# Moving parts within the instruction queues of a two-layer graph network: walk products ahead of the searches' parts, transposes in one run, loads on another engine, later side work

## The chip, the cores and the metric

The kernel runs on one core of one Trainium2 chip. The time is the device time of one execution in microseconds (us). It was run three times, and the median counts. One further execution was profiled; the profile and its trace come from that one.

## The reference, cut to what matters

A graph of N = 2708 nodes with D = 256 features passes through two layers. `x` is (2708, 256), `adj` (2708, 2708); all is float32.

```python
# layer 0: two steps of attention and of a random walk
R = adj + eye;  R = R / R.sum(-1)
Xf = Xa = x;  Z = 0
for n in range(2):
    q, k = Xa @ W1.T @ W2.T, Xa @ W3.T            # width 64
    probs = softmax(q @ k.T)                      # (2708, 2708)
    A = probs cut to the fewest largest values of a row whose sum reaches 0.9
    A = A / A.sum(-1)
    Xf, Xa = R @ Xf, A @ Xa
    Z = Z + Xf @ U1[n].T + Xa @ U2[n].T
x = layernorm(x + layernorm(x + Z) * g + b)
# layer 1: graph attention of 4 heads, width 64 each
Wh = einsum('nd,hdo->nho', x, W)
e = leaky_relu(s_i[:, None, :] + s_j[None, :, :], 0.2)   # s from Wh and a
att = softmax(where(adj != 0 or i == j, e, -inf), axis=1)
x = layernorm(x + einsum('ijh,jho->iho', att, Wh))
```

## The kernel before, in words

**Tiles.** The rows are cut into 22 tiles (`NT`): 16 of 128 rows and 6 of 110. Tiles of one height are taken in six groups of 4, 4, 4, 4, 4 and 2 (`groups`). TensorE (PE) makes all products; ScalarE (ACT) exponentials, copies and sums; VectorE (DVE) the searches; GpSimd (POOL) small sums; SyncE (SP) starts most DMAs. `manual_schedule` keeps PE, ACT, DVE and POOL in the order in which the program issues, one block for layer 0 and one for layer 1; SP is not among them.

**Opening.** `turn_x` (L1080) transposes x into `x_turned` (which lies in `ba`), group by group: four tiles by two halves c of the features, the halves side by side in one PSUM tile `lg`. ACT copies the half c = 0 and DVE the half c = 1 (L1091). `project` makes the queries and keys (L631) one group behind.

**Steps of layer 0.** A *search* (`search`) finds for one tile of rows which probabilities are kept. It is a generator in parts: `scores` (products L661, exponentials L665), `survey` (tallies on ACT, L686, and POOL), `bound` (a pass of DVE over the row, L751), `candidates` (L766), `settle` (L779-L838; its last pass, L835, leaves the values that the attention product transposes). The first step's searches have no survey. `step(s, ...)` goes through the tiles; for each tile, `weigh` takes the six groups: transposes of the next group (L240), ACT's copy `eT` (L245), products with the values (`att`, L258), and then `between(n)`, which ends in one call of `slot`. So a tile has six slots, n = 0 to 5. In slot 4 the search of the tile three further on is begun.

A slot drives three lists. `going` holds the searches and `doing` the smaller finishing jobs; `advance` takes each a part further. `stream` is the *random walk*, `walks`: 22 products L901 to each tile of R, read in blocks `blk` from HBM. A slot takes a given number of them (`spend`: 7 between the steps, 7 or 6 counted pieces a slot in the second). A walk's 22nd product appends the job `after_walk0` (first step) or `finish` (second step) and runs its first part at once: the DVE add that reads the walk's only PSUM bank (L915 with reciprocal L916, or L974). Its second part, at the next `advance(doing)`, is work for POOL (L918, L919) or ACT (L976) and POOL.

```python
            advance(going)
            if begin and begin[1] < NT:
                ...
            advance(doing)
            owed[0] += spend
            while owed[0] > 0: ...        # the walk's products
```

**Layer 1.** For each pair of a source tile j and a span of 8, 8 or 6 target tiles: the mask (`neighbours`: adj block loaded by SP, then Sign and Square on ACT, L1221/L1222), four weight tiles `pt` on DVE (L1302), products with `v` (L1313) and with the denominators (L1323) on PE. `mask(n)` runs three pairs ahead and `weights(n)` two; in the first span `mask` also loads `v[j]` (L1290). The loop makes two pairs an iteration and calls `beside` twice. `beside` carries side work: the last four tiles of layer 0 (`LATE`), whose layer norms and sources are made by `prepared` (ACT L145, L148, L153, POOL, then transposes L160 and products L166 on PE, exponentials and copies L162-L176 and a DMA L179 on ACT), and `verdict`, a check of the searches. Each of these has a count of calls before it starts.

**Buffers.** Each pool takes a stretch of on-chip memory in the order in which it is opened; layer 1's pools lie over those of layer 0, which are closed.

Of the kernel before, what the change touches and what calls it, by code (L numbers as in the profile page):

```python
# [37 lines left out]
HELD, WAITING = 6, 4  # L38
# [6 lines left out]
def kernel(  # L45
# [16 lines left out]
    nc = tc.nc  # L62
# [5 lines left out]
    NT = (N + P - 1) // P  # L68
# [48 lines left out]
    LATE = 4  # L117
# [37 lines left out]
    def sources(t, pool, room, queue=nc.sync):  # L155

        m = rows[t]
        tp = room()
        for c in range(DC):
            nc.tensor.transpose(tp[:, c, :m], xe[:m, t, c * P : (c + 1) * P], ident[:m, :m])  # L160
        xT = pool.tile([P, DC, P], F32, name="xT")
        nc.scalar.copy(xT[:, :, :m], tp[:, 0:DC, :m])  # L162
        yield
        wp = room().rearrange("p a b -> p (a b)")
        for c in range(DC):
            nc.tensor.matmul(  # L166
                wp[:m, : D + 2 * H], xT[:, c, :m], wx[:, c, :],
                start=(c == 0), stop=(c == DC - 1),
            )
        nc.scalar.activation(sb[:m, t, :], wp[:m, D : D + H], AF.Exp)  # L170
        nc.scalar.activation(tj[:m, t, :], wp[:m, D : D + H], AF.Exp, scale=NEG_SLOPE - 1.0)
        nc.scalar.copy(s_src[:m, t, :], wp[:m, D + H : D + 2 * H])
        vt = pool.tile([P, D], F32, name="cs")
        for h in range(H):
            cols = slice(h * FO, (h + 1) * FO)
            nc.scalar.activation(  # L176
                vt[:m, cols], wp[:m, cols], AF.Copy, scale=sb[:m, t, h : h + 1]
            )
        queue.dma_start(vd[t][:m], vt[:m])  # L179

    def norms(t, xt, norm=layernorm, other=None):

        m = rows[t]
        hh = xe[:m, t, 0:D]
        h2 = hh if other is None else other()[:m]
        yield from norm(h2, hh, m)
        nc.gpsimd.tensor_mul(h2, h2, g_sb[:m])  # L187
        nc.gpsimd.tensor_add(h2, h2, xt[:m])  # L188
        yield
        yield from norm(hh, h2, m)  # L190
        yield
        if t < NT - LATE:
            yield
# [331 lines left out]
    def fast_layer0(ep, adjp):  # L525

        l0 = ExitStack()

        heldp, finp, rowp, w0, keep, tpp, sortp, keepb, wk = (
            l0.enter_context(tc.tile_pool(name=name, bufs=bufs))  # L530
            for name, bufs in (
                ("heldp", HELD), ("finp", 2), ("rowp", 2), ("w0", 1), ("keep", 1),
                ("tpp", 3), ("sortp", 1), ("keepb", 1), ("wk", 1),
            )
        )
        ps_lg, ps_wk, ps_at, ps_tr = (
# [304 lines left out]
        def search(s, t):  # L841

            e, z, tau = yield from scores(s, t)
            if s:
                seen = yield from survey(t, e, z, tau)
                src, rest = bound(t, e, z, tau, *seen)
            else:
                src, rest = e, tau
            yield
            cand = yield from candidates(s, t, src)  # L850
            yield
            ready[t] = e, (yield from settle(s, t, e, cand, rest))
# [138 lines left out]
        stream = walks()  # L991
        owed = [0]

        def advance(parts):
            for g in list(parts):
                if next(g, parts) is parts:
                    parts.remove(g)

        def slot(spend, begin=None):

            advance(going)
            if begin and begin[1] < NT:
                going.append(search(*begin))
                next(going[-1])
            advance(doing)
            owed[0] += spend
            while owed[0] > 0:
                owed[0] -= 1
                if next(stream, True):
                    break  # L1010

        def step(s, cur, spend):
            first = None
            for t in range(NT):
# [11 lines left out]
                def between(n):  # L1026
                    last = n == len(groups) - 1
                    if last:
                        xa = heldp.tile([P, D], F32, name="xa1")
                        nc.scalar.activation(xa[:m], ac[:m, :D], AF.Copy, scale=rden)  # L1030
                        if s and t in c3:
                            nc.gpsimd.dma_start(c3[t][:m], xa[:m])
                            stored.add(t)
                        elif s:
                            held[t] = xa
                        else:
                            doing.append(after_attention0(t, xa))
                    slot(spend[n], (s, t + 3) if n == len(groups) - 2 else None)
# [41 lines left out]
        def turn_x(grp):  # L1080
            k = rows[grp[0]]
            w, c0 = k * len(grp), off[grp[0]]
            tp = ps_lg.tile([P, 2, CHUNK], F32, name="lg")
            for c in range(DC):
                for q, t in enumerate(grp):
                    nc.tensor.transpose(
                        tp[:, c, q * k : (q + 1) * k], xm[:k, t, c * P : (c + 1) * P],
                        ident[:k, :k],
                    )
                copy = nc.vector.tensor_copy if c else nc.scalar.copy  # L1090
                copy(x_turned[:, c, c0 : c0 + w], tp[:, c, :w])  # L1091
            return c0, w

        with tc.manual_schedule(engines=engines):
            query_weights()
            ahead = turn_x(groups[0])
            for n in range(len(groups)):
# [3 lines left out]
                pj = ps_tr.tile([P, 4, P], F32, name="tr").rearrange("p a b -> p (a b)")  # L1101
# [5 lines left out]
            for n in range(10):  # L1107
                slot(0, (0, n // 4) if n in (0, 4, 9) else None)
                for t in range(n * NT // 10, (n + 1) * NT // 10):
                    terms1(t, x_turned[:, :, off[t] : off[t + 1]])  # L1110
            layer1_weights()
            step(0, xm, [0] * len(groups))
            while doing:
                slot(SPEND_BETWEEN)
# [78 lines left out]
    def layer1(ep, adjp, r=None, verdict=None):  # L1193
        l1 = ExitStack()

        pp, pj, rp, keep = (
            l1.enter_context(tc.tile_pool(name=name, bufs=bufs))
            for name, bufs in (("pp", 2), ("pj", 1), ("rp", 1), ("keep1", 1))
        )
        DEEP = 3  # L1200
        ps_u = l1.enter_context(tc.tile_pool(name="ps_u", bufs=2, space=PSUM))
# [12 lines left out]
        def neighbours(g, j):  # L1214

            k = rows[j]
            i0, i1 = off[spans[g][0]], off[spans[g][-1] + 1]
            bar = adjp.tile([P, NT - HT, P], F32, name="blk")
            bar = bar.rearrange("p t d -> p (t d)")[:k, : i1 - i0]
            nc.sync.dma_start(bar, adjT[off[j] : off[j + 1], i0:i1])  # L1220
            nc.scalar.activation(bar, bar, AF.Sign)  # L1221
            nc.scalar.activation(bar, bar, AF.Square)  # L1222
            if j in spans[g]:
                own = bar[:, off[j] - i0 : off[j + 1] - i0]
                nc.vector.tensor_tensor(own, own, ident[:k, :k], op=ALU.max)
            return bar
# [59 lines left out]
        def mask(n):  # L1286
            if n < len(order):
                g, _, j = order[n]
                if g == 0:
                    nc.sync.dma_start(  # L1290
                        v[j][: rows[j]].rearrange("p h o -> p (h o)"), vd[j][: rows[j]]
                    )
                masks[n] = neighbours(g, j)
# [36 lines left out]
        def prepared(t):  # L1330

            yield from norms(
                t, x_late[:, t - NT + LATE, :], layernorm_beside,
                lambda: pp.tile([P, D], F32, name="h2", bufs=4),
            )
            yield from sources(t, pp, aux, nc.scalar)


        late = []
        if verdict:  # L1340
            late += [[k, prepared(NT - LATE + k)] for k in range(LATE)]
            late.append([LATE, verdict(aux)])
        rest, running = [], []
        def beside(g, i):

# [19 lines left out]
        for n in range(DEEP):  # L1365
            mask(n)
# [3 lines left out]
        for n in range(0, len(order), 2):  # L1370
            g, i, j = order[n]
            beside(g, i)
            weights(n + 2)
            mask(n + 3)
            if i == 0:
                acc = [
# [7 lines left out]
            for u in (n, n + 1):  # L1384
                for k in range(2):
                    values(u, (2 * k, 2 * k + 1))
                    if last and u > n:
                        for c, (c0, w) in enumerate(cuts[g]):
                            copy = nc.scalar.copy if c == 0 else nc.vector.tensor_copy
# [3 lines left out]
            if last:  # L1393
                for c, (c0, w) in enumerate(cuts[g]):
                    copy = nc.scalar.copy if c == 0 else nc.vector.tensor_copy
# [3 lines left out]
            else:  # L1399
                beside(g, i + 1)  # L1400
            weights(n + 3)
            mask(n + 4)
        assert not late

# [10 lines left out]
    with ExitStack() as both:  # L1415

        adjp = both.enter_context(tc.tile_pool(name="adjp", bufs=3))
        ep = both.enter_context(tc.tile_pool(name="ep", bufs=3))
        left = fast_layer0(ep, adjp)
        with tc.manual_schedule(engines=engines):  # L1420
            layer1(ep, adjp, *left)
    flag = nc.values_load(bad[0:1, 0:1])
    with tc.If(flag > 0):
        general_layer0()
        with ExitStack() as again:
            adjp = again.enter_context(tc.tile_pool(name="adjp", bufs=3))
            ep = again.enter_context(tc.tile_pool(name="ep", bufs=3))
            layer1(ep, adjp)
# [45 lines left out]
```

## Time and profile before

| What | Value |
|---|---|
| Median of three runs | 1595.95 us (1595.8 to 1597.88) |
| Profiled execution, its own time | 1593.14 us |
| Its span, first to last instruction | 1591.3 us |
| Mean granted TensorE clock | 0.990 |
| Busy: PE / DVE / ACT / POOL | 1542.3 / 1202.5 / 798.9 / 429.1 us |
| Opening to the first scores of layer 0 | about 0 to 34 us |
| First step, then between the steps | to about 446, then to 523 us |
| Second step | 523 to 1229 us |
| Layer 1 | from 1229 us |

The table reads the profiled execution, except for its first row. Busy times overlap, as the engines run beside each other. The page cuts the span in 40 slices of 39.8 us, and a digit gives the busy share of an engine in one. The list of waits puts each idle stretch of an engine down to the work that ended it; a timeline gives start, length, line and tiles of runs of instructions, and in brackets the idle time before them with what ended it. "SPq" and "ACTq" are SP and ACT at starting DMAs.

### The profile page before, as it was taken

Reading aid. Unit: us, or ns where it says so; the run is one execution under the profiler, and the core shown is the slowest. Engines: PE = TensorE matmul, PEld = TensorE weight load, DVE = VectorE, ACT = ScalarE, POOL = GpSimd, SP = SyncE. Lnnn points to the kernel's source line nnn. Section 1 sums busy time; section 2 is a strip of 40 time slices with the busy share of each in tenths; the row PEclk is TensorE's granted clock in tenths of the full one; section 3 lists DMA queues with packets and bytes.
Section 4 is the critical chain, followed back from the end, with each engine's and each line's share of the span. In section 5 each row is a group of like instructions: output and inputs, shape, how many; then the busy total and the mean of one; then the engine's idle time right before and its main releaser. Section 6 shows DMA issues by size and latency. Waiting matters only on the chain. (4 is left out here: it accounts for less than half of the span.)

```text
span 1591.3 us, 23822 instructions
## 1 busy us (share of the span) xinstructions
PE 1542.3 (97%) x8029; PEld 1037.7 (65%) x8029; DVE 1202.5 (76%) x3651; ACT 798.9 (50%) x1462; POOL 429.1 (27%) x884
## 2 busy tenths in 40 slices
PE   6999999999998999999999999999999999999994
PEld 3477777777776888787787788887787333333342
DVE  2777677767408876878779888888884978999995
ACT  2444444444335455555555556556643454456473
POOL 1311000000022222232224454534441720033133
PEclk9999999999999999999999999999999999999997
DMA  5200000000134333333333334433344434334331
GB/s 139 78 13 14 12 9 12 10 9 10 42 94 124 86 100 82 98 76 78 80 102 94 100 107 107 111 104 93 78 101 130 130 102 139 93 105 133 85 100 43
DMA packets 172494, 128.27 MB, mean 81 GB/s; under 512 B 44342, under 2 KB 161804, under 8 KB 172362
## 3 DMA queue, kind: packets, MB, share of 16 engines
q1 hardware_dynamic: 165030, 114.63, 26.9%
q0 software_dynamic: 3648, 9.26, 1.8%
q10 hardware_dynamic: 3684, 2.76, 0.5%
q8 instruction: 65, 1.06, 0.3%
q14 instruction: 67, 0.55, 0.1%
HBM read 111.78 MB, written 13.46 MB: 79 GB/s over the span
## 5 line engine op out<-in xcount | busy, mean ns | idle before, releaser
L245 ACT COPY eT<-tr 128x512 f32<-128x512 f32 (+5 forms) x264 | 141.2, 535 | 275.8 <-PE tr L240 273.1
L686 ACT ACTIVATE junk<-e,minus,rth 128x2708 bf16<-128x2708 f32 (+1 forms) x88 | 232.8, 2646 | 36.1 <-POOL rth L718 35.2
L258 PE MATMUL att<-xm,eT 128*128 128x256 f32 (+3 forms) x968 | 230.9, 380 | 0.4 <-ACT xa L1030 0.4
L258 PE MATMUL att<-ba,eT 128*128 128x256 f32 (+3 forms) x968 | 230.8, 379 | 0.3 <-ACT eT L245 0.2
L901 PE MATMUL walk<-xe,blk 128*128 128x257 f32 (+3 forms) x968 | 225.3, 384 | 5.0 <-DVE xf L915 5.0
L901 PE MATMUL walk<-xm,blk 128*128 128x256 f32 (+3 forms) x968 | 222.0, 380 | 1.0 <-DVE xw L974 1.0
L1313 PE MATMUL acc<-pt,v 128*64 128x512 f32 (+3 forms) x1056 | 216.3, 555 | 2.4 <-DMA v<-v 2.2
L901 PEld LDWEIGHTS walk<-xe,blk 128*128 128x128 f32 (+3 forms) x968 | 178.5, 187 | 50.3 <-issue 12.6
L1302 DVE SCALAR_TENSOR_TENSOR pt<-e,tj,blk 128x1024 f32<-128x1024 f32 (+3 forms) x176 | 187.1, 1128 | 20.3 <-PE att L258 8.7
L901 PEld LDWEIGHTS walk<-xm,blk 128*128 128x128 f32 (+3 forms) x968 | 177.7, 186 | 34.5 <-issue 4.9
L258 PEld LDWEIGHTS att<-xm,eT 128*128 128x128 f32 (+3 forms) x968 | 169.6, 186 | 22.1 <-ACT xa L1030 0.8
L258 PEld LDWEIGHTS att<-ba,eT 128*128 128x128 f32 (+3 forms) x968 | 169.5, 186 | 22.0 <-ACT eT L245 0.8
L665 ACT ACTIVATE e<-lg 128x1024 f32<-128x1024 f32 (+1 forms) x132 | 121.0, 921 | 110.6 <-PE lg L661 107.0
L1313 PEld LDWEIGHTS acc<-pt,v 128*64 128x64 f32 (+1 forms) x1056 | 75.6, 139 | 133.2 <-issue 107.5
L766 DVE MAX8 cand<-e 128x8 f32<-128x170 f32 (+1 forms) x352 | 89.6, 323 | 90.5 <-ACT e L665 90.4
L240 PEld LDWEIGHTS tr<-ident,e 128*128 128x128 f32 (+3 forms) x968 | 115.1, 138 | 56.3 <-issue 21.0
L240 PE MATMUL tr<-ident,e 128*128 128x128 f32 (+3 forms) x968 | 147.1, 271 | 0.7 <-ACT xe L952 0.3
L1302 DVE SCALAR_TENSOR_TENSOR pt<-r,tj,blk 128x1024 f32<-128x1024 f32 (+1 forms) x88 | 110.0, 1313 | 5.8 <-PE acc L1323 3.0
L1323 PE MATMUL acc<-pt,sb 128*32 128x512 f32 (+3 forms) x1056 | 106.8, 545 | 0.0
L766 DVE MAX8 cand<-scr 128x8 f32<-128x97 f32 (+1 forms) x616 | 102.3, 245 | 0.0
L1221 ACT ACTIVATE blk<-blk 128x1024 f32<-128x1024 f32 (+3 forms) x66 | 63.1, 956 | 70.2 <-DMA blk<-in_adjT_dram 57.1
L915 DVE TENSOR_TENSOR xf<-walk,xe 128x257 f32<-128x257 f32 (+1 forms) x22 | 9.4, 426 | 110.8 <-PE walk L901 110.8
(237 smaller groups left out, 1976.2 us busy)
## 6 DMA issues: line engine op xcount, KB each, us to landing
blk<-in_adjT_dram SPq DMA_DIRECT2D x32, 704.0 KB
blk<-in_adjT_dram SPq DMA_DIRECT2D x32, 512.0 KB
blk<-in_adjT_dram SPq DMA_DIRECT2D x48, 330.0 KB
blk<-in_adjT_dram SPq DMA_DIRECT2D x32, 320.0 KB
blk<-in_adjT_dram SPq DMA_DIRECT2D x12, 605.0 KB
blk<-in_adjT_dram SPq DMA_DIRECT2D x12, 440.0 KB
blk<-in_adjT_dram SPq DMA_DIRECT2D x18, 283.6 KB
c<-cs POOLq DMA_DIRECT2D x32, 128.0 KB, 2.0
```

The source lines that it names most:

```text
L240: nc.tensor.transpose(tr[: rows[t], q, :m], e[:m, off[t] : off[t + 1]], ident[:m, :m])
L245: copy(eT[:k, : len(grp), :m], tr[:k, : len(grp), :m])
L258: nc.tensor.matmul(acc, eT[: rows[t], q, :m], value(t), start=(t == 0), stop=(t == NT - 1),)
L665: nc.scalar.activation(halves[:m, :, c0 : c0 + w], lg[:m, :, :w], AF.Exp, accum_out=zp[:m, n : n + 1],)
L686: nc.scalar.activation(junk[:m], e[:m], func, scale=rth, bias=minus1[:m], accum_out=acc)
L766: nc.vector.max(cand[:, n, :], src[:m, n * size : min(N, (n + 1) * size)])
L901: nc.tensor.matmul(ac[:m, :w], blk[: rows[j], j - j0, :m], cur[: rows[j], j, 0:w], start=(j == 0), stop=(j == NT - 1),)
L915: nc.vector.tensor_add(xf[:m], ac[:m, : D + 1], xe[:m, t, :])
L1221: nc.scalar.activation(bar, bar, AF.Sign)
L1302: nc.vector.scalar_tensor_tensor(pt[:k, :gw], targets[g][h // 2][:k, h % 2, :gw], tj[:k, j, h : h + 1], bar, op0=ALU.max, op1=ALU.mult,)
L1313: nc.tensor.matmul(acc[h // 2][c][q * FO : (q + 1) * FO, :w], v[j][:k, h, :], probs[n][h][:k, c0 : c0 + w], **at,)
L1323: nc.tensor.matmul(acc[2][c][h * 32 : (h + 1) * 32, :w], sb[:k, j, h : h + 1].to_broadcast([k, 32]), probs[n][h][:k, c0 : c0 + w], **at,)
```

## The change

There are five edits. The pools of layer 0 and of layer 1 are opened in another order, so that their addresses move. In `slot` the products of the walk come ahead of the searches' parts and the other jobs. In `turn_x` all eight transposes of a group are issued ahead of the two copies. In layer 1 the loads of `v` are started by ACT and not SP. The late parts of `prepared` start after twice as many calls of `beside`: tiles 18 to 21 at call 0, 2, 4, 6 and not 0, 1, 2, 3, and `verdict` after 8 calls and not 4.

```diff
--- before.py
+++ after.py
@@ -526,11 +526,11 @@
 
         l0 = ExitStack()
 
-        heldp, finp, rowp, w0, keep, tpp, sortp, keepb, wk = (
+        heldp, finp, rowp, tpp, w0, keep, sortp, keepb, wk = (
             l0.enter_context(tc.tile_pool(name=name, bufs=bufs))
             for name, bufs in (
-                ("heldp", HELD), ("finp", 2), ("rowp", 2), ("w0", 1), ("keep", 1),
-                ("tpp", 3), ("sortp", 1), ("keepb", 1), ("wk", 1),
+                ("heldp", HELD), ("finp", 2), ("rowp", 2), ("tpp", 3), ("w0", 1),
+                ("keep", 1), ("sortp", 1), ("keepb", 1), ("wk", 1),
             )
         )
         ps_lg, ps_wk, ps_at, ps_tr = (
@@ -998,16 +998,16 @@
 
         def slot(spend, begin=None):
 
+            owed[0] += spend
+            while owed[0] > 0:
+                owed[0] -= 1
+                if next(stream, True):
+                    break
             advance(going)
             if begin and begin[1] < NT:
                 going.append(search(*begin))
                 next(going[-1])
             advance(doing)
-            owed[0] += spend
-            while owed[0] > 0:
-                owed[0] -= 1
-                if next(stream, True):
-                    break
 
         def step(s, cur, spend):
             first = None
@@ -1087,7 +1087,7 @@
                         tp[:, c, q * k : (q + 1) * k], xm[:k, t, c * P : (c + 1) * P],
                         ident[:k, :k],
                     )
-                copy = nc.vector.tensor_copy if c else nc.scalar.copy
+            for c, copy in enumerate((nc.scalar.copy, nc.vector.tensor_copy)):
                 copy(x_turned[:, c, c0 : c0 + w], tp[:, c, :w])
             return c0, w
 
@@ -1193,9 +1193,9 @@
     def layer1(ep, adjp, r=None, verdict=None):
         l1 = ExitStack()
 
-        pp, pj, rp, keep = (
+        pp, rp, pj, keep = (
             l1.enter_context(tc.tile_pool(name=name, bufs=bufs))
-            for name, bufs in (("pp", 2), ("pj", 1), ("rp", 1), ("keep1", 1))
+            for name, bufs in (("pp", 2), ("rp", 1), ("pj", 1), ("keep1", 1))
         )
         DEEP = 3
         ps_u = l1.enter_context(tc.tile_pool(name="ps_u", bufs=2, space=PSUM))
@@ -1287,7 +1287,7 @@
             if n < len(order):
                 g, _, j = order[n]
                 if g == 0:
-                    nc.sync.dma_start(
+                    nc.scalar.dma_start(
                         v[j][: rows[j]].rearrange("p h o -> p (h o)"), vd[j][: rows[j]]
                     )
                 masks[n] = neighbours(g, j)
@@ -1338,8 +1338,8 @@
 
         late = []
         if verdict:
-            late += [[k, prepared(NT - LATE + k)] for k in range(LATE)]
-            late.append([LATE, verdict(aux)])
+            late += [[2 * k, prepared(NT - LATE + k)] for k in range(LATE)]
+            late.append([2 * LATE, verdict(aux)])
         rest, running = [], []
         def beside(g, i):
```

## The prediction

> **What bounds the kernel now.** First the page's busy slices, then the whole list of TensorE's waits (line, releaser, total, times, longest):
>
> ```profile
> PE   6999999999998999999999999999999999999994
> DVE  2777677767408876878779888888884978999995
> PEclk9999999999999999999999999999999999999997
> ...
> PE lg L1086 <- ACT ba L1091: 6.4, 6, 1.6
> PE walk L901 <- DVE xf L915: 5.0, 3, 3.2
> PE tr L610 <- DMA xa<-in_w1T_dram: 4.8, 1, 4.8
> PE aux L166 <- ACT xT L162: 3.8, 2, 2.1
> PE acc L1313 <- DMA v<-v: 2.2, 1, 2.2
> PE tr L631 <- ACT qT L636: 1.6, 2, 1.0
> PE aux L160 <- ACT xe L153: 1.1, 1, 1.1
> PE walk L901 <- DVE xw L974: 1.0, 2, 0.8
> ```
>
> TensorE is busy 1542.3 us of 1591.3, and its waits add to about 28 us. No matmul is added or removed, so the change acts through these few waits, the new ones that it makes, and the clock. By windows, the opening 0-40 us holds 13.2 us of TensorE's idle time, 400-600 some 6, 1200-1300 some 7, the tail 1560-1592 20.9 (untouched). A gain on TensorE before 1230 carries on: from 40 to 446 it has no gap to swallow it.
>
> The granted clock, read in stretches of a few us, falls to half four times after the opening, for 3.4 us each: from 515.2, 1232.0, 1283.2 and 1300.3, just after TensorE gaps of 3.18, 2.19, 2.05 and 1.74 us. Gaps of 1.15 and 1.32 us did not do it. One costs about 1.65 us.
>
> **What the Trainium skill says.** "TensorE: Matmul & The Clock Gate", section "What's actually happening": the clock halves after one idle window of some 3.4 us, and the windows run free. The trace agrees on the 3.4 us that a half clock lasts, but here gaps of 1.74 us, half a window, were enough; I follow the trace. "Perfetto Trace Analysis", section "Tensor Engine Instruction (MATMUL, LD_WEIGHTS)": ACT's and DVE's queues are strictly first in, first out. The trace agrees: small adds on DVE stand behind 3 us passes. "DMA: Bandwidth & Descriptors", section "Issuing engines are not separate DMA queues": starting DMAs from several engines saves only issue time. Here an issue holds SP 0.43 us and ACT 0.29-0.57. The same page, section "Anatomy of one DMA — SWDGE (gpsimd) path", has a semaphore wait served on the issuing sequencer ahead of dispatch; the trace agrees: SP stood 8.7 us in front of the v loads.
>
> **Part 1, the pools' order.** Only addresses move. The pools of layer 1 that matter (v's and the weights' own) still overlap `ba` or `keep`, which the last attention product reads, so first writes wait for the same end (1229.3). 0, or ±0.5.
>
> **Part 2, the transposes of the opening (L1086).**
>
> ```profile
> 18.21 0.66 PE L1086 MATMUL lg<-ident,xm 128*128 128x128 f32 x4 [1.18 <-ACT ba L1091]
> ...
> 22.58 0.66 PE L1086 MATMUL lg<-ident,xm 128*128 128x128 f32 x4 [1.56 <-ACT ba L1091]
> ```
>
> The second four transposes of every group wait for ACT's copy of the first, as the tile is shared. Six such waits: 0.68+0.68+1.18+1.56+0.89+1.45 = 6.44. All eight ahead of both copies removes them. Late next are the copies: DVE's still follows ACT's, and `project` (L631) waits for it, one group later. Stepping the six groups through with the traced durations, the last L631 ends near 29.6 instead of 34.17: **-4.5** (-3.5 to -6; 2 of the 6.4 come back as waits for copies).
>
> **Part 3, slot: walk products first.** Between the steps (446-523):
>
> ```profile
> 510.95 3.04 DVE L751 SCALAR_TENSOR_TENSOR scr<-e,hi 128x2708 f32<-128x2708 f32 x1
> ...
> 514.30 0.42 DVE L915 TENSOR_TENSOR xf<-walk,xe 128x257 f32<-128x257 f32 x1
> ```
>
> The add that frees the walk's bank stands behind bound's pass of 3.04 us; TensorE waits 3.18 us, then runs at half clock. With the add ahead of the search's part, waits of 5.0 fall to 0.8-1.3 and the half clock (1.65) goes: about -4.5 (with some 0.9 held back). The xw waits (1.0) and the L644 wait (0.6), covered by walk products, go too: **-6.1**.
>
> In step 1 (523-1229) the same move turns the queue round. A slot's TensorE work (4 transposes, 8 attention products, 14 walk products at 0.2275) is 5.21 us, issued without a break. DVE runs ahead now, finishing its searching before the walk ends, and then waits idle:
>
> ```profile
> 744.66 0.43 DVE L915 TENSOR_TENSOR xf<-walk,xe 110x257 f32<-110x257 f32 x1 [1.90 <-PE walk L901]
> ```
>
> After, this add stands first, and in slot 4 of a tile the next tile's final pass (L835, 3.04+0.08 us) stands behind it. That pass writes the values which TensorE transposes at the beginning of slot 5. With the walk's end at T, the add (0.42), the reciprocal (0.17) and the pass end at T+3.7 to 3.85. After T TensorE has only the survey's scores, 1.95-2.0, and at times 0.35 of transposes. It stands 1.35-1.9 us. Of the 22 walks, those ending in a slot 4 with a final behind are the ones with adds at 744.66, 911.94, 945.57 and 1117.29: 1.9+1.4+1.75+1.4 = 6.45. Walks ending in slot 3 ahead of a full slot 4 (706.60, 1075.33) add 0.45 and 0.2-0.9: 7.8 in all. Gaps from 1.7 us on bring the half clock about half the time: two of four, 2 × 0.5 × 1.65 = 1.7. The other moved instructions: ACT's scale L976 and POOL's L918/919 come into the queues with slack (the next eT copy is a slot away): 0. Search DMAs on POOL and SP do not cross the walk's loads in another order that a wait shows: 0.
>
> Part 3: -6.1 + 7.8 + 1.7 = **+3.4** (-4 to +12: none of the new waits, or all with half clocks and DVE late into the next slot).
>
> **Part 4, the v loads issued by ACT (L1290).**
>
> ```profile
> 1229.40 5.80 DVE L1302 SCALAR_TENSOR_TENSOR pt<-e,tj,blk 128x1024 f32<-128x1024 f32 x4 [8.67 <-PE att L258]
> ...
> 1206.89 1.06 ACT L1221 ACTIVATE blk<-blk 128x1024 f32<-128x1024 f32 x1 [2.22 <-DMA blk<-in_adjT_dram]
> 1207.98 1.06 ACT L1222 ACTIVATE blk<-blk 128x1024 f32<-128x1024 f32 x1
> ...
> 1229.33 4.67 SPq L1290 DMA_DIRECT2D v<-v  x10
> ```
>
> Today ACT makes the first three masks (Sign, Square) at 1206.9-1225.8, before the last attention product, and DVE starts the first weights 0.07 after it. A v load must wait for that product, as v's tiles lie over `ba`. On ACT it stands ahead of its tile's Sign, and ACT keeps the written order: Sign 0 then starts only after the load. So the first weights start at 1229.3 + 0.47 (xa copy) + 0.4 (issue) + 2 × 1.06 = 1232.3 instead of 1229.40. TensorE's 2.19 us wait for v goes, but it now waits for the weights. The first iteration is DVE-paced (1231.5-1245.5, against 10.6 later), so nearly all of it counts: **+2.5** (0 to +4). Behind it ACT has the layer norms of the late tiles.
>
> **Part 5, late parts at twice the calls (L1341).** Today the late tiles' POOL chain runs back to back 1241-1275, and TensorE waits 1.15 + 2.05 + 1.74 = 4.94 at L160/L166, with two half clocks (3.2). Those go. New ones come: each tile's step with L166, the exponentials and the DMA now falls on an odd call, the next tile's Identity (L153) follows it on ACT in that call, and its transposes L160 stand first on TensorE at the next call.
>
> ```profile
> 1280.21 0.93 ACT L176 ACTIVATE cs<-aux,sb 110x64 f32<-110x64 f32 x4
> 1281.17 0.57 ACTq L179 DMA_DIRECT2D v<-cs  x1
> ...
> 1282.02 0.60 ACT L153 ACTIVATE xe<-h,lb_nb,lb_rs 110x256 f32<-110x256 f32 x1
> ```
>
> Three tiles wait some 1.15 + 0.57 + 0.6 = 2.3 (2.45, 2.2, 2.2: 6.9), and two in three bring the half clock (3.3): 6.9 + 3.3 - 4.94 - 3.2 = **+2.1** (-5 to +6: the low end if ACT, less crowded, ends them in time). The verdict, 4 calls later, is off the path: 0.
>
> **Sum**: -4.5 + 3.4 + 2.5 + 2.1 + 0 = **+3.5**. The profiled execution took 1593.14 (span 1591.3 and 1.84 around it), so 1596.6; the median of the runs is 1595.95, 2.81 above that execution, and the same step gives **1599.5**. A measurement here tells about 0.2% (3.2 us) from no change: faster is under 1592.8, slower over 1599.1.
>
> **Rivals.**
> A, one more cover: the searches' finals are ready before the walk ends, since DVE was ahead, and the first masks are not held. For it: DVE's slices in step 1 read 7 to 8 tenths, so it has slack on average. Against: final and add stand in the same slot, whichever slack there is elsewhere. Taking off half of 9.5 and the 2.5: -3.7, about 1592. With layer 1's late chain also free (-5 for part 5 instead of +2.1): 1585.
> B, no difference: only parts 4 and 5 miss. Then -4.5 + 3.4 ≈ -1.1: 1595 to 1598. For it: the v wait and the late waits vanish as meant. Against: ACT's order.
> C, the other way and further: every new TensorE stand of 1.4-2.4 us (four in step 1, three in layer 1) is answered with a 3.4 us half clock, and a late DVE meets the next slot's 5.8 us settle pass. It decides from gaps of 1.7 us. 7 × 1.65 - 5.0 counted = +6.5: 1606, up to 1612 with DVE's lag.
> That the change doesn't act: if the shared tile still makes transposes wait across groups, part 2 gives -1 instead of -4.5 and the sum is +7: 1606.5.
>
> **How the numbers follow.** The forecast's own case 0.45, of which 0.37 on the slow side of 1599.1 and 0.08 within the bound; A 0.18; B 0.19; C and no action 0.18. So faster 0.18, same 0.27, slower 0.55. The range 1591-1612 leaves out A's lower half and worse than C.
>
> **What would show it.** Right: no wait at L1086 for L1091; none at L901 for L915; new waits of TR L240 for DVE L835 of 1.3-1.9 at four places; Sign 0 of layer 1 behind 1229.3, first weights near 3 us after the last attention product; L160 waiting for L153 three times. Wrong: TensorE without new waits between 523 and 1229, or Sign 0 still ahead of the last attention product, or step 1 longer by more than 12 us.

## The result, and the profile after

The changed kernel takes 1611.45 us (median of 4 runs, 1610.32 to 1612.23) against 1595.88 for the kernel before on the same chip: a ratio of 1.0095, 95% interval 1.0077 to 1.0112. It is slower by some 15 us. Its profiled execution has a span of 1610.4 us, 19.1 more than before, and a mean TensorE clock of 0.985, as have its three other runs. The spans differ by more than the medians because the profiled execution before was 2.8 us faster than its median.

The page's slices of the changed kernel, each 40.3 us long:

```profile
PE   8999999999998999999999989999898989999995
DVE  4677777777117877777888877888783888999995
```

TensorE's eights in the 24th, 29th, 31st and 33rd slice (from 926, 1127, 1208 and 1288 us) were nines before: two places in step two, the boundary to layer 1, and the late tiles there. The list of TensorE's waits names them:

```profile
PE att L258 <- ACT eT L245: 7.6, 2, 3.8
PE aux L160 <- ACT xe L153: 6.5, 3, 2.2
PE tr L240 <- DVE e L835: 5.9, 6, 1.9
PE tr L240 <- ACT cs L176: 5.5, 1, 5.5
PE tr L610 <- DMA xa<-in_w1T_dram: 4.8, 1, 4.8
PE acc L1313 <- DVE pt L1302: 4.1, 1, 4.1
PE walk L901 <- DVE xf L915: 2.8, 4, 1.3
PE tr L631 <- ACT qT L636: 2.1, 2, 1.6
```

Gone are the 6.4 us at L1086, the waits at L166 in layer 1 and the 2.2 for `v`; the waits for the walk's add are down from 6.0 to 2.8. The second, third and sixth line are new and were forecast. The first and the fourth were not: the attention's products wait for ACT's copy `eT`, or its transposes for the copies that stand ahead of that one, three times, for 3.75, 3.83 and 5.48 us.

I lined up the slots of both traces by the start of their transposes (L240). The difference, after less before, grows like this:

| Stretch | Difference, us |
|---|---|
| Opening, to the first scores (34.10 to 25.66) | -8.4 |
| Between the steps, to the last slot's end | -5.2 |
| First slot of step two (wait of 3.75, then half clock) | +6.5 |
| Slot near 940 (wait of 3.83, half clock), without its L835 wait | +7.3 |
| Slots near 1155 (wait of 5.48, half clock) | +7.1 |
| Six waits for L835 | +5.9 |
| All else in step two | +1.1 |
| Layer 1 | +4.8 |
| Sum, as the spans have it | +19.1 |

So 21 us come from three places that the forecast had at nothing. The one near 940 can be followed from engine to engine. This is the timeline of the changed kernel:

```profile
921.69 0.42 DVE L974 TENSOR_TENSOR xw<-walk,xm 128x256 f32<-128x256 f32 x1 [3.98 <-PE walk L901]
922.04 0.19 DVE L779 TENSOR_REDUCE fact<-cand 128x1 f32<-128x28 f32 x1
...
928.00 0.26 DVE L795 TENSOR_SCALAR_CACHE_REDUCE sums<-top,fact 128x48 f32<-128x48 f32 x1
...
928.87 0.15 DVE L133 TENSOR_SCALAR ln_ve<-ln_mv 128x1 f32<-128x1 f32 x1
...
929.10 0.55 POOL L135 TENSOR_TENSOR ln_rs<-ln_ve,minus_half 128x1 f32<-128x1 f32 x1 [8.51 <-DVE need L804]
929.61 0.72 POOL L979 TENSOR_TENSOR xe<-ca,cb 128x256 f32<-128x256 f32 x1
...
931.98 0.73 POOL L982 TENSOR_TENSOR ca<-ca,b_sb 128x256 f32<-128x256 f32 x1
...
934.79 0.19 POOL L718 TENSOR_TENSOR rth<-rth,g 128x1 f32<-128x1 f32 x1
...
935.01 2.64 ACT L686 ACTIVATE junk<-e,minus,rth 128x2708 bf16<-128x2708 f32 x1 [10.42 <-POOL rth L718]
937.65 0.56 ACT L245 COPY eT<-tr 110x512 f32<-110x512 f32 x1
...
938.27 3.78 PE L258 MATMUL att<-ba,eT 110*128 110x256 f32 x8 [3.83 <-ACT eT L245]
```

DVE stands 3.98 us in front of the walk's add. Only then come the settle part (922.04 to 928.2) and, behind it in the same queue, the statistics of a layer norm that another job wants (L129 to L133). POOL has already arrived at that layer norm's L135 and waits 8.51 us. (The list names DVE's L804; the value that L135 reads is L133's, which ends just before it.) Behind L135, POOL has four adds (3.0 us) and the bounds L712 to L718 (2.3). ACT waits 10.42 us for them, as the next instruction in its own queue is the tally L686, and the copy that TensorE needs stands behind that. TensorE then takes 3.78 us for eight products that need 1.89 at the full clock. In the kernel before, at the same place:

```profile
924.16 0.26 DVE L795 TENSOR_SCALAR_CACHE_REDUCE sums<-top,fact 128x48 f32<-128x48 f32 x1
...
926.78 0.42 DVE L974 TENSOR_TENSOR xw<-walk,xm 128x256 f32<-128x256 f32 x1 [2.02 <-PE walk L901]
...
929.36 2.64 ACT L686 ACTIVATE junk<-e,minus,rth 128x2708 bf16<-128x2708 f32 x1 [1.55 <-POOL rth L718]
...
934.59 0.59 ACT L245 COPY eT<-tr 110x512 f32<-110x512 f32 x1 [1.09 <-PE tr L240]
```

There DVE does the settle part first (it ends at 924.4) and waits for the walk when nothing is urgent; the tally starts 1.55 us after ACT is free, and the copy waits for TensorE and not the other way round.

### The profile page after: what moved, and what is told of

It reads as the page before. It is cut to its first block, busy times and chain, and to the rows that moved or that the text cites. A ratio compares the mean times of both kernels' runs of the same rounds, so it can differ in the third digit from the quotient of the medians.

```text
span 1610.4 us, 23811 instructions
## 1 busy us (share of the span) xinstructions
PE 1547.4 (96%) x8029; PEld 1042.0 (65%) x8029; DVE 1203.3 (75%) x3651; ACT 793.2 (49%) x1462; POOL 446.2 (28%) x884
## 5 line engine op out<-in xcount | busy, mean ns | idle before, releaser
L686 ACT ACTIVATE junk<-e,minus,rth 128x2708 bf16<-128x2708 f32 (+1 forms) x88 | 232.9, 2647 | 77.5 <-POOL rth L718 76.6
L258 PE MATMUL att<-ba,eT 128*128 128x256 f32 (+3 forms) x968 | 236.3, 386 | 7.6 <-ACT eT L245 7.6
L901 PEld LDWEIGHTS walk<-xm,blk 128*128 128x128 f32 (+3 forms) x968 | 181.0, 187 | 29.9
L240 PEld LDWEIGHTS tr<-ident,e 128*128 128x128 f32 (+3 forms) x968 | 112.0, 139 | 81.4 <-issue 33.4
L240 PE MATMUL tr<-ident,e 128*128 128x128 f32 (+3 forms) x968 | 149.0, 273 | 12.2 <-DVE e L835 5.9
L784 DVE MAX8 top<-work 128x8 f32<-128x128 f32 (+3 forms) x242 | 82.4, 340 | 8.3
```

Of the source, the lines that this page charges most:

```text
L240: nc.tensor.transpose(tr[: rows[t], q, :m], e[:m, off[t] : off[t + 1]], ident[:m, :m])
L258: nc.tensor.matmul(acc, eT[: rows[t], q, :m], value(t), start=(t == 0), stop=(t == NT - 1),)
L686: nc.scalar.activation(junk[:m], e[:m], func, scale=rth, bias=minus1[:m], accum_out=acc)
L784: nc.vector.max(top[:, k : k + 8], work if k else flat)
L901: nc.tensor.matmul(ac[:m, :w], blk[: rows[j], j - j0, :m], cur[: rows[j], j, 0:w], start=(j == 0), stop=(j == NT - 1),)
```

## The experiments

Ratios are to the kernel before on the same chip, with 95% intervals. Its median was 1593.4 to 1597.0 from one chip to the next, so the ratios are compared, not the times. Theory V is the chain just shown. Theory P, which I held first, puts the loss on POOL's jobs, standing a slot earlier than before.

**The opening alone** (`c_only`): in `turn_x`, all eight transposes ahead of both copies, as in the diff of the change.

```diff
-                copy = nc.vector.tensor_copy if c else nc.scalar.copy
+            for c, copy in enumerate((nc.scalar.copy, nc.vector.tensor_copy)):
```

> The transposes' run of the opening alone (L1086 to L1091). In the changed kernel's trace the first scores start at 25.66 us, against 34.10 before: 8.4 us. Theory: TensorE is dense from there to the end, so the whole of it reaches the end: 1595.9 - 8.4 = 1587.5 us, ratio 0.9947. Rival: part of it came from the other edits (the v loads or the pools' addresses can't reach the opening, but a later stage could swallow some of it): 4.5 as forecast, 1591.4, ratio 0.9972.

Measured 0.9933 (0.9915 to 0.9951), 10.7 us; the span is 9.3 shorter, and the first scores start 9.2 earlier (24.92). The whole of the gain arrives at the end, and the 4.5 of the forecast were too few.

**The slot's order alone** (`b_only`).

```diff
+            owed[0] += spend
+            while owed[0] > 0: ...
             advance(going)
             ...
             advance(doing)
-            owed[0] += spend
-            while owed[0] > 0: ...
```

> The order in a slot alone: the walk's products first. By the changed kernel's trace it gains 5.2 us between the steps and loses 27.9 behind them. Theory (the slot's order carries the loss by itself): 1595.9 + 22.7 = 1618.6, ratio 1.014, with three waits of 3.7 to 5.5 us of TensorE that end with a copy on ScalarE behind a tally (L686), each followed by half clock. Rival (the loss comes from where the earlier opening puts the work against the loads and the windows of the clock): near the forecast of +3.4, ratio 1.002.

Measured 1.0114 (1.0093 to 1.0134). The same three waits stand at the same places, of the same lengths (3.8, 3.8 and 5.5). These losses belong to this edit and don't depend on the opening. The ratio is below the 1.014 of the expectation, which was worked out from spans; the span is 22.5 us longer, as expected.

**Layer 1's two edits alone** (`de_only`, both), and **the v loads alone** (`d_only`, the first).

```diff
-                    nc.sync.dma_start(
+                    nc.scalar.dma_start(          # v[j]
 ...
-            late += [[k, prepared(NT - LATE + k)] for k in range(LATE)]
-            late.append([LATE, verdict(aux)])
+            late += [[2 * k, prepared(NT - LATE + k)] for k in range(LATE)]
+            late.append([2 * LATE, verdict(aux)])
```

> The v loads on ScalarE and the late parts at twice the calls, without the others. Forecast +4.6; the changed kernel's trace has 4.8 more us behind the last attention product. Theory: both are local to layer 1, so 1600.6, ratio 1.003, with three waits of L160 for L153 of about 2.2 us and first weights 2.7 us after the last attention product. Rival: part of the 4.8 is an effect of the later searches that run into it; then 1596 to 1598, ratio 1.000 to 1.001.

> The v loads of layer 1 issued by ScalarE, without the other edits. The forecast has +2.5: first weights 2.7 us behind the last attention product (0.07 before), with TensorE's wait of 2.2 for v replaced by one of 4.1 for the weights: net 1.9. Theory: 1.9, ratio 1.001. Rival: nothing, as VectorE catches up where TensorE has later waits: ratio 1.000.

Measured 1.0003 (0.9992 to 1.0015) for both and 1.0014 (1.0007 to 1.0021) for the v loads, which is 2.2 us. The first is nearer to the rival's number, though its trace has every wait of the forecast (4.2 for the weights, 6.5 for L153). In the changed kernel's trace:

```profile
1243.63 0.35 ACTq L1290 DMA_DIRECT2D v<-v  x1
1244.17 1.06 ACT L1221 ACTIVATE blk<-blk 128x1024 f32<-128x1024 f32 x1
1245.26 1.06 ACT L1222 ACTIVATE blk<-blk 128x1024 f32<-128x1024 f32 x1
...
1246.35 16.83 DVE L1302 SCALAR_TENSOR_TENSOR pt<-e,tj,blk 128x1024 f32<-128x1024 f32 x14 [11.34 <-ACT blk L1222]
...
1247.69 10.30 PE L1313 MATMUL acc<-pt,v 128*64 128x512 f32 x32 [4.11 <-DVE pt L1302]
```

The load waits for the last attention product (it ends at 1243.6), the first mask waits behind the load, the weights behind the mask. The wait of 4.1 takes the place of one of 2.2.

**Jobs a slot later** (`s1_jobs_late`): the slot's order as in the change, but a job's second part stays where it was.

```diff
+            earlier, owed[0] = list(doing), owed[0] + spend
             (walk products)
             advance(going)
-            advance(doing)
+            [doing.remove(job) for job in earlier if next(job, doing) is doing]
```

> Walk products first in a slot, and the walk's add on VectorE ahead of the search's part as in the change, but a job's second part (POOL's L918/L919, ScalarE's L976 and POOL's four adds) stays a slot later, where it stood before. Theory P (POOL's jobs ahead of the next search's bounds L672/L712 to L718 make the tally on ScalarE late, and the attention's copy behind it): the three long waits go or shrink below 2 us, the 5.9 us for L835 stay, the 5 us between the steps are gained: 1595.9 - 6 + 6 to 10 = 1596 to 1600, ratio 1.000 to 1.003. Rival V (VectorE, held by the add until the walk ends, is late with the settle and the layer norm that POOL waits for, wherever POOL's jobs stand): like the slot order alone, 1610 to 1619, ratio 1.009 to 1.014.

Measured 1.0213 (1.0189 to 1.0236): slower than either theory said, and against P. TensorE's waits for ACT are more, not fewer, and by the same chain:

```profile
905.81 0.55 POOL L135 TENSOR_TENSOR ln_rs<-ln_ve,minus_half 128x1 f32<-128x1 f32 x1 [5.55 <-DVE need L804]
...
911.56 2.64 ACT L686 ACTIVATE junk<-e,minus,rth 128x2708 bf16<-128x2708 f32 x1 [9.48 <-POOL rth L718]
...
915.37 0.68 PE L240 MATMUL tr<-ident,e 128*110 128x128 f32 x2 [3.32 <-ACT cs L176]
```

Six tallies start 8.4 to 9.8 us after ACT is free, against two (10.4 and 10.7) in the changed kernel. The layer norms moved by a slot as well, so this run doesn't test POOL's jobs by themselves. Which slot a job falls in matters, but not in the way that P had it.

**Jobs behind the walk, searches ahead of it** (`s6_jobs_behind`).

```diff
             advance(going)
             ...
-            advance(doing)
             (walk products)
+            advance(doing)
```

> A slot goes: searches' parts, walk products, jobs. So TensorE's scores and VectorE's settle stand ahead of the walk and its add, as before; alone the jobs come behind the walk, and the second part of a walk's job (POOL's L918/L919 or four adds) one slot earlier, as in the change. Theory V (the losses at 945 and 1161 come from VectorE's settle standing behind the add that waits for the walk): no wait of the attention for a tally's copy, waits of 5 us between the steps as before: 1594 to 1599, ratio 0.999 to 1.002. Theory P (POOL's jobs standing a slot earlier): waits of 3.7 us and more near 945 and 1161 with half clock, 1605 to 1612.

Measured 1.0004 (0.9992 to 1.0015). POOL's jobs stand a slot earlier, as in the change, and no product waits more than 0.2 us for `eT`, as before. So P falls. As the searches' scores on TensorE also stand ahead of the walk here, this run doesn't tell VectorE's order from TensorE's; the next one does.

**TensorE's order alone** (`s2_pe_only`): walk products first, the add issued at the end of the slot.

```diff
                         doing.append(after_walk0(t, ac, ca) if s == 0 else ...)
-                        next(doing[-1])
+                        pass
```

> Walk products first in a slot for TensorE alone: the add at a walk's end (L915, L974) is issued at the end of the slot, so that VectorE, ScalarE and POOL keep the order of before. Theory: the loss of 5 us just behind the boundary of the steps (first attention of the second step waiting for a copy behind a tally) comes from TensorE's order, as the last scores of tile 2 go behind 14 walk products (3.2 us): it stays. The losses at 945 and 1161 come from VectorE's order: they vanish, and so do the waits for L835. New: the next walk's first product now waits for an add behind bound or settle, 1 to 3 us in some of 40 slots. 1600 to 1612, ratio 1.003 to 1.010. Rival (all three come from VectorE's order): no wait for a tally at all.

Measured 1.0106 (1.0083 to 1.0129), just above the upper end. The losses near 940 and 1155 and the waits for L835 are gone, so these come from VectorE's order: from the add ahead of the searches' part. The price is paid elsewhere:

```profile
PE walk L901 <- DVE xf L915: 10.5, 4, 5.2
PE walk L901 <- DVE xw L974: 3.8, 3, 2.2
PE att L258 <- ACT eT L245: 2.2, 2, 1.8
```

The next walk begins at once in the next slot and needs the add. Of the 5 us at the boundary of the steps, which I expected to stay, only 1.5 are left, so TensorE's order alone doesn't make that loss, at least not with the walk itself 9 us later.

**Without the layer norms** (`b_no_norms` and `no_norms`): the slot's order of the change and that of before, both without the norms of tiles 0 to 17.

```diff
-                yield from norms(t, ca)
+                yield from (None for _ in range(5))
```

> The slot order alone, leaving out the two layer norms of layer 0 for its first 18 tiles (VectorE's L129 to L137, POOL's L135, L187, L188); the number of parts of a job is kept. Theory V in full (VectorE held by the add, the settle behind it, then the layer norm's L133, then POOL's L135 that waits for it, and behind L135 the bounds L712 to L718 that the tally waits for): the waits near 945 (8.5 us with its half clock) and 1161 (7) go, the 5.2 at the boundary of the steps and the 5.9 for L835 stay: 1615.4 - 15.5 = 1600, ratio 1.003. Rival (the tallies are late without the layer norm, through the four adds of POOL or the settle itself): 1610 to 1616, ratio above 1.008.

> The kernel before, leaving out the same two layer norms of layer 0 for its first 18 tiles. It is the base for the run of the slot order without them: TensorE's waits of before name no layer norm, so theory V has no change, 1593 to 1597, ratio 0.998 to 1.001, and the slot order then costs some 2 us without the layer norms where it costs 18 with them. Rival: leaving them out is worth 10 us or more by itself (VectorE and POOL freed): ratio below 0.994, and the comparison proves nothing.

Measured 1.0009 (0.9996 to 1.0022) with the change's order and 0.9983 (0.9975 to 0.9990) with the old one. So the slot's order costs 0.26% without the norms and 1.14% with them: some 14 of 18 us hang on the layer norm. TensorE's waits of the former:

```profile
PE tr L240 <- DVE e L835: 5.9, 6, 1.9
...
PE att L258 <- ACT eT L245: 3.8, 1, 3.8
```

The six waits for L835 stay, the one at the boundary stays, the two others are gone. Near 940 the tally starts 4.2 us after ACT is free, where it had been 10.4:

```profile
937.31 2.64 ACT L686 ACTIVATE junk<-e,minus,rth 128x2708 bf16<-128x2708 f32 x1 [4.17 <-POOL rth L718]
```

With the run of TensorE's order alone, this shows theory V for both places in the middle of step two. Leaving the norms out takes their own work from POOL and DVE as well as their waiting; that the waiting is the larger part (8.51 us at L135, against some 2.5 us of POOL's work on the norms of a tile) is read from the trace.

**Late parts at odd calls** (`e_odd`): calls 1, 3, 5, 7, with no other edit.

```diff
-            late += [[k, prepared(NT - LATE + k)] for k in range(LATE)]
-            late.append([LATE, verdict(aux)])
+            late += [[2 * k + 1, prepared(NT - LATE + k)] for k in range(LATE)]
+            late.append([2 * LATE + 1, verdict(aux)])
```

> The kernel before with the late parts of prepared started at calls 1, 3, 5, 7 (the change: 0, 2, 4, 6; before: 0, 1, 2, 3), verdict after 9. The Identity L153 then falls on an even call with TensorE's products behind it before the transposes L160 come. Theory: no wait of L160 for L153, a wait of L166 for L162 of 0.4 to 0.8 per tile, no half clock from them; against the 4.9 us and two half clocks of before: 1596.6 - 5 = 1591.6, ratio 0.997. Rival: part of a few us is swallowed by the weights on VectorE, which pace these iterations: 1595 to 1597, ratio 0.999 to 1.000.

Measured 0.9959 (0.9943 to 0.9976), 6.5 us. Four tiles' products now wait 0.3 to 0.5 us each; the waits for L153 are gone, and so are the half clocks behind the late tiles' waits. (The half clock behind the wait for `v` is gone too, though that wait, 2.1 us, is still there.)

```profile
1294.35 1.14 PE L166 MATMUL aux<-wx,xT 128*110 128x264 f32 x4 [0.43 <-ACT xT L162]
```

The change doubled the distance between tiles, but put them all at even calls, where the next tile's Identity (L153) meets the transposes with no product between them.

**Versions that beat both.** `best_open_late` has the opening's edit and the odd calls; `best_early` has another order of the slots between the steps as well:

```diff
+            (between the steps: the newest search's part)
+            (walk products)
+            (the older searches' parts)
             advance(doing)
```

> The kernel before with the run of transposes of the opening (-10.4 measured, 0.9933) and the late parts at calls 1, 3, 5, 7 (0.9959). The two lie 1200 us apart with TensorE dense between: they should add, ratio 0.989. Rival: the clock's windows or the loads shift with the opening and give back some: 0.992 to 0.994.

> The kernel of the previous run with another order of the slots between the steps only: first the newest search's part (scores, which need nothing of VectorE), then the walk's products with their add, then the older searches' parts (bound, settle), then the jobs. The second step keeps the slots of before. Theory: the walk's add no longer stands behind bound (5.0 us of waits and a half clock of 1.65 go), the scores are not later, so the loss of 5 us at the boundary stays away, and step two has VectorE ahead as before: a further 5 us, ratio 0.986. Rival: older searches' parts behind the add are late for the first attention of step two, by the 1 to 3 us of the pass L835: ratio 0.988 to 0.990.

Measured 0.9891 (0.9875 to 0.9906) for the first, 1578.8 us: the ratios of its two parts multiply to 0.9892, so the gains add. The second, at 0.9895 (0.9879 to 0.9910), is no better: the new order between the steps gains 5.9 us there and loses 7.1 in the first slot of step two. Its timeline shows the boundary's loss without a late score:

```profile
501.39 0.72 ACT L665 ACTIVATE e<-lg 128x660 f32<-128x660 f32 x1 [0.97 <-PE lg L661]
...
501.73 3.02 DVE L835 SCALAR_TENSOR_TENSOR e<-scr,fact,e 128x2708 f32<-128x2708 f32 x1
...
501.92 3.64 POOL L918 TENSOR_SCALAR xf<-xf,rinv 128x256 f32<-128x256 f32 x1 [9.04 <-DVE rinv L916]
...
506.68 3.04 DVE L751 SCALAR_TENSOR_TENSOR scr<-e,hi 128x2708 f32<-128x2708 f32 x1
...
506.88 2.93 POOL L675 TENSOR_SCALAR tau<-fact 128x1 f32<-128x1 f32 x1
...
514.20 2.07 PE L258 MATMUL att<-ba,eT 128*128 128x256 f32 x4 [4.43 <-ACT eT L245]
```

The scores are done at 502.1. POOL, though, has the walk's job L918 ahead of the search's L672 to L699, and an instruction of it that starts beside a long pass of DVE ends only behind that pass: 3.64 us for L918 (0.94 elsewhere), 2.93 for L675 (0.23). ACT's tally starts 8 us after ACT is free, and the copy follows it.

In the changed kernel two things meet at this place. The last scores come late, at 507.6, as 18 walk products of TensorE (501.9 to 506.0) stand ahead of them; L918 takes 3.64 us there too, but POOL then still waits for these scores. And the search's L673 starts beside DVE's pass L751:

```profile
507.86 2.16 POOL L673 TENSOR_TENSOR fact<-fact,zp 128x1 f32<-128x1 f32 x1 [1.09 <-ACT e L665]
```

It takes 0.19 us elsewhere. In `s2_pe_only` the scores were as late (they end 2.3 us ahead of the first transposes of step two, in both runs), but L673 met no pass and took 0.19, TensorE waited 1.78 us and not 3.75, and the loss was 1.5. In `s1_jobs_late` POOL had the search ahead of L918, the scores were late, L673 took 2.07, and the loss was 5.1. So late scores alone cost little here; most of the loss came where a small instruction of POOL was held beside a pass of DVE as well, and half clock followed. What an order without both would give was not tried.

## Why the prediction was right or wrong

The direction was right and the time lay at the upper end of the range; the size was not right: +3.5 forecast, 15.6 measured. That the time lay inside the range, by half a microsecond, was luck: the upper end was made for other losses than those that came. By the prediction's own sign ("step 1 longer by more than 12 us", its name for the second step) its mechanism failed there: that stretch grew by 28 us.

- **Opening.** -4.5 forecast, -8.4 in the trace. Two terms were mis-sized. "2 of the 6.4 come back as waits for copies": the copies came in time (the one wait for `qT` grew from 1.05 to 1.60). And the "traced durations" were partly those of a slow clock: TensorE is at half speed at first, to about 17 us in the kernel before (four transposes take 1.02 us at 16.0 and 0.60 at 20.4) and to about 12 in the changed one. By this, and in part by their unbroken runs, the transposes take 7.2 us together and not 9.0, and the first projection (L631) takes 2.46 and not 3.62: 3.0 us in all. The four traces with the new opening reach full speed at 10.7 to 12.2 us, the ten others at 14.8 to 17.9. The changed kernel, then the kernel before:

```profile
7.55 3.67 PE L1086 MATMUL lg<-ident,xm 128*128 128x128 f32 x16
11.02 2.46 PE L631 MATMUL tr<-ba,wkqk 128*128 128x512 f32 x4
...
12.59 3.62 PE L631 MATMUL tr<-ba,wkqk 128*128 128x512 f32 x4
```

- **Between the steps.** -6.1 forecast, -5.2 measured: right.
- **Step two, waits for L835.** Forecast 7.8 in six places, measured 5.9 in six: mechanism right, size a third too large. The half clock added to them, 1.7, did not come: these gaps, of up to 1.9 us, left the clock alone.
- **Step two, what else moves.** This is the step that failed: "The other moved instructions ... come into the queues with slack (the next eT copy is a slot away): 0." I had followed the add into TensorE's transposes, not into the rest of the chain: settle, the layer norm's statistics, POOL's queue, the tally and the copy. Each of these has slack for itself, but POOL and ACT work in order, and together they ran more than a slot late. Worth 14.4 us in two places; 6.5 more came at the boundary, from late scores and POOL's held L673. The rule was in the prediction, from the Trainium skill's page "Perfetto Trace Analysis", section "Tensor Engine Instruction (MATMUL, LD_WEIGHTS)", for ACT and DVE; I applied it to one queue and not to four in a row.
- **The v loads.** +2.5 forecast, 1.9 by the waits, 2.2 by the run.
- **Late parts.** Three waits of L160 for L153 were forecast with 6.9 and came with 6.5; two of the three brought a half clock, as forecast. The waits they replace were 4.9. The net, +2.1 in the forecast, is -1.8 from the two ratios (1.0003 less 1.0014), with intervals that allow about ±2; its sign isn't settled.
- **Pools.** Not run alone. The ratios of the three parts that were (opening, slot, layer 1) multiply to 1.0049 against 1.0095, which leaves some 7 us, with intervals that only just meet. Most of this is half clock. By estimate a mean clock of 0.985 over 1610 us, as in all four runs of the change, stands for 24 us of lost work, and the 0.988 to 0.989 of the slot's order alone for 18; the two other parts had 0.990 to 0.993, much like the kernel before (0.989 to 0.994). That is some 6 of the 7 us. In the profiled executions half clock lasted 6.8 us at the boundary of the steps in the changed kernel and 3.4 in the slot's order alone, and fell three times in the first part of layer 1 and not at all. Why stays open: the pools' addresses, or the moments at which the waits fall when the parts meet.

Of the rivals, C named the right side and price (1606 to 1612) with the wrong mechanism: of the seven gaps that it multiplied, the four of step two did not halve the clock, two of the three in layer 1's late tiles did, and the larger gaps came from elsewhere. The sum of the last rival was wrong as well: +7 on the median of 1595.95 is 1603, not 1606.5.

## What to carry to other kernels

When an instruction that waits is put ahead of work on an in-order engine, follow everything behind it through all the queues until it comes back to the engine that sets the end, here VectorE to GpSimd to ScalarE to TensorE; slack in each queue by itself was no cover. An add that may wait belonged behind the work that others need; between the steps, where its own consumer could not afford that, the place ahead of it gained 5.2 us up to the boundary. Side work that hands over between engines did best with a stretch of the main engine's work between each hand-over: at the same doubled spacing, odd calls gained 6.5 us and even calls 1.8, give or take 2. And durations read where the clock is still slow should not be carried over to a change that lets it rise earlier.

## What the runs showed of the hardware

- A GpSimd instruction that computes and starts beside a VectorE pass with two full-size inputs (L751 or L835) ends only behind the pass: L918 took 3.64 us beside L835 and 0.94 elsewhere, L135 3.27 in five places and 0.55 elsewhere, in both kernels. The Trainium skill's page "SBUF — State Buffer", section "Terms", has the cause that fits: the two engines share a pair of memory ports under an exclusive lock, held for a whole instruction. The trace agrees; I had not drawn on it. GpSimd's issue of a DMA was not held: L1032 took 0.67 us beside L751 in the changed kernel, as elsewhere.
- The length of a wait did not settle what the clock did behind it. The kernel before had gaps of 2.19, 2.05 and 1.74 us in layer 1, each with 3.4 us of half clock behind it; the slot's order alone had gaps of 2.18, 2.05 and 1.74 at the same places, and none. A wait of 3.75 us at the boundary of the steps had 6.8 us behind it in the changed kernel, and 3.4 in the slot's order alone; the wait of 3.2 there had 3.4 in the profiled execution before and 6.8 in that of the v loads alone. So one gap's price differs by some 1.7 us between executions, and a single span can't show a difference of that size.
